# The queue's part between the two pairs of maxima, VectorE held in the source's order, and FP4 quantization in three steps

## The chip, the core and the metric

The kernel runs on one core of a Trainium2 chip. Its engines work side by side, each through its own queue of instructions: PE (TensorE, matmuls, with PEld for the loading of weights), DVE (VectorE), ACT (ScalarE), POOL (GpSimd) and SP (SyncE, which issues most DMAs). The metric is the device time of one execution in microseconds, taken as the median of several runs.

## What is computed

One transformer layer in float32: x has 4 batches of 2048 rows of 256. Attention with 16 heads of 16, residual and layer norm, then a gated feed-forward with FP4 quantization of activations and weights, residual and layer norm.

```python
q, k, v = (split_heads(x @ W.T) for W in (Wq, Wk, Wv))
attn = softmax(einsum('bhld,bhmd->bhlm', q, k) / sqrt(16))
x = layernorm(x + merge(attn @ v) @ Wo.T)
gate, y = fp4_linear(x, w_gate), fp4_linear(x, w_up)       # 256 -> 704
x = layernorm(x + fp4_linear(silu(gate) * y, w_down))      # 704 -> 256
# fp4_linear quantizes both operands in blocks of 16:
scale = max(|block|) / 6;  q = nearest of 0, .5, 1, 1.5, 2, 3, 4, 6 times scale
```

## The kernel before

**Steps and periods.** Attention is cut into 64 steps: a batch, a block of 512 query rows and a group of four heads. A step has 16 periods, so there are 1024 of them, and the loop at L860 writes them out, n from -20 to 1025. Four steps, 64 periods, make a block of query rows. In a period a step gets 128 rows further in each of three stages, which belong to different steps:

- *maxima* (L417), 20 periods ahead (LEAD): the scores of 128 query rows against 512 keys, for a pair of heads at a time. A pair is two matmuls (pm) of 62 rows of contraction, in the two halves of the array. VectorE reduces both banks to row maxima (mx, L432). There are two pairs in a period, here called m0 and m1; pm has two buffers.
- *exponentials* (L458): the transposed scores of 128 keys, two pairs of matmuls (pe) of 64 rows, here e0e1 and e2e3, with ScalarE's exponential after each (e, L466).
- *values* (L469), two periods behind (LAG): av, four heads side by side, eight matmul records.

**The queue's part.** All other work is cut into parts by generators that yield: projections of q, k and v (pq, pv, with transposes ptx), the output projection (py), the feed-forward (ptq, pg, pu, pth, pz) and the preparation of the FP4 weights (`prepare`, L265). `period` (L819) first runs what is due, then the urgent generators (`max_rows`, pn; `normalize`, pa and pr), then as many parts of the queue as are still free: one in a period, two before n = 0. A part counts if it yields at least LEAST = 300. A generator that waits for something also yields LEAST: the period then has no part. On TensorE the part comes last; it is called F here. Each next block's `chain` joins the queue when a block of query rows has its values.

**Due work.** `later(periods, step, rest)` (L117) puts a step into a period to come and returns a test that becomes true `rest` periods after the step ran. `fp4` (L146) uses it: block maxima (amax), scale (sc), its reciprocal (rs) and the scaled rows (xn, on POOL) at once, the rounding (m on VectorE, three operations on POOL) one period later.

**Order.** TensorE's instructions are held in the order of the source by `matmul` and `transpose` (L134, L137). Those of VectorE, ScalarE, POOL and SP are put in order by the framework, from the dependences and its own estimate of when an engine is free.

**Memory.** Three PSUM banks (px) serve pe and all parts in turn, four serve pm, one av. The weights' pieces (wl) have one buffer: ten pieces, loaded by SP in `load` (L278), quantized and transposed into place during the first block. k tiles are loaded in every fourth period, for the step two ahead, into 16 buffers, so SP waits there for the step that is just running.

**The end.** After the loop L900 empties the queue, and `feed_forward_last` (L678) does the last block of rows by itself.

Of the kernel before, what the change touches and what calls it, by code (L numbers as in the profile page):

```python
# [38 lines left out]
P = 128  # L39
# [13 lines left out]
LEAD = 20  # L53
LAG = 2
E_BUFS = 10
LEAST = 300.0
# [15 lines left out]


@with_exitstack
def block_kernel(
# [11 lines left out]
):  # L87
    nc = tc.nc
    B, L, D = x.shape
    FF = w_gate.shape[0]  # L90
# [55 lines left out]
    def fp4(pool, t, tag, gain=1.0):  # L146

        p, nb, _ = t.shape
        amax = pool.tile([p, nb], F32, tag="amax" + tag, name="amax")
        nc.vector.tensor_reduce(amax, t, AX.X, ALU.max, apply_absolute_value=True)  # L150
        sc = pool.tile([p, nb], F32, tag="sc" + tag, name="sc")
        nc.vector.tensor_scalar(sc, amax, gain / 6.0, 1e-12, ALU.mult, ALU.max)
        rs = pool.tile([p, nb], F32, tag="rs" + tag, name="rs")
        nc.vector.reciprocal(rs, sc)
        nc.gpsimd.tensor_scalar(rs, rs, gain * TIES_DOWN, 1.0, ALU.mult, ALU.mult)
        xn = pool.tile([p, nb, FB], F32, tag="xn" + tag, name="xn", bufs=3 if tag else 2)
        nc.gpsimd.tensor_tensor(xn, t, rs.unsqueeze(2).to_broadcast([p, nb, FB]), ALU.mult)

        def rounded():
            m = pool.tile([p, nb, FB], F32, tag="m" + tag, name="m", bufs=1)  # L160
            nc.vector.tensor_single_scalar(m.bitcast(I32), xn.bitcast(I32), EXPONENT, ALU.bitwise_and)
            nc.vector.tensor_scalar(m, m, 1.0, ROUND, ALU.max, ALU.mult)  # L162
            nc.gpsimd.tensor_tensor(xn, xn, m, ALU.add)  # L163
            nc.gpsimd.tensor_tensor(xn, xn, m, ALU.subtract)  # L164
            nc.gpsimd.tensor_tensor(xn, xn, sc.unsqueeze(2).to_broadcast([p, nb, FB]), ALU.mult)  # L165

        return xn, later(1, rounded, 4 if tag == "" else 2)

# [75 lines left out]
    def turn_w(name, dst):  # L244
        for kc in range(KC):
            pt = psum("ptw")
            for n in range(KC):
                transpose(pt[:, n * P : (n + 1) * P], loaded[name][:, n, kc * P : (kc + 1) * P], ident)
            if name == "wv":
                nc.vector.tensor_copy(dst[:, kc, :], pt[:, :D])  # L250
                continue

            for n in range(KC):
                nc.vector.tensor_copy(
                    dst[:, kc, n * P : (n + 1) * P].rearrange("p (d h) -> p d h", h=NC),
                    pt[:, n * P : (n + 1) * P].rearrange("p (h d) -> p d h", h=NC),
                )
# [7 lines left out]
    def prepare():  # L265
# [9 lines left out]
        nc.scalar.copy(woT.rearrange("p k n -> p (k n)"), pt)  # L275
        yield 500

# [36 lines left out]
        for piece, after in zip(pieces, pieces[1:] + [None]):  # L314
            following = load(*after) if after else None
            yield from transposed(*piece, *q)
            q = following
            yield 500

# [13 lines left out]
    def project(b, tb, what):  # L333
# [7 lines left out]
        for kc in range(KC):  # L341
# [4 lines left out]
            yield 600  # L346
        for name, c in [(w[0], int(w[1])) for w in what if w != "v"]:
            w, dst = (wkT, kx[b % 2][c][:, :, rows]) if name == "k" else (wqT, qx[(b * NQB + tb) % len(qx)][c])
# [16 lines left out]
            projected.add((b, tb, name + str(c)))  # L365
        for t in range(QT if "v" in what else 0):
            v = vt[(tb * 2 + t // 2) % 4]
            pv = psum("pv")
            for kc in range(KC):
                matmul(  # L370
                    pv[:, :D], xT[:, kc, t * P : (t + 1) * P], wvT[:, kc, :], start=(kc == 0), stop=(kc == KC - 1)
                )
            src = pv[:, :D].rearrange("p (g i j d) -> p g i j d", g=NG, i=NP, j=2)
            for j in range(2):
                nc.scalar.copy(v[:, :, t % 2, :, 2 * j * DH : (2 * j + 1) * DH], src[:, :, :, j, :])
            if t % 2:
                t0 = tb * QT + t - 1
                nc.sync.dma_start(
                    vx[b % 2][:, :, t0 : t0 + 2, :].rearrange("g p t c -> p g (t c)"),
                    v.rearrange("p g t i c -> p g (t i c)"),  # L380
                )
            if t == QT - 1:
                projected.add((b, tb, "v"))
            yield 900

# [31 lines left out]
    def maxima(s, n, i):  # L417
# [5 lines left out]
        for j in range(2):  # L423
# [7 lines left out]
            )  # L431
        nc.vector.tensor_reduce(mx_sb[s][:, t, 2 * i : 2 * i + 2, kb], pm, AX.X, ALU.max)  # L432

    def max_rows(s):

        nm = p2.tile([P, QT, HG], F32, tag="nm", name="nm")
        nc.vector.tensor_reduce(nm, mx_sb.pop(s), AX.X, ALU.max, negate=True)
        nh = p2.tile([P, QT, HG, 2], F32R, tag="nh", name="nh")
        nc.vector.tensor_copy(nh[:, :, :, 0], nm)
        nc.vector.tensor_tensor(nh[:, :, :, 1], nm, nh[:, :, :, 0].bitcast(F32), ALU.subtract)  # L440
        yield 0
# [15 lines left out]

    def exponentials(s, kt, i):  # L458
        kb, col = kt // QT, kt % QT * P
        pe = [psum("pe") for _ in range(2)]  # L460
        for j in range(2):
            rows = slice(R * j, R * j + R)
            matmul(pe[j], k_sb[s, i, kb][rows, col : col + P], q_sb[s, i][rows, :], start=True, stop=True)
        for j in range(2):
            e = p1.tile([P, QB], F32, tag="e", name="e", bufs=E_BUFS)
            nc.scalar.activation(e, pe[j], AF.Exp, scale=SCALE)  # L466
            e_sb[s, kt, 2 * i + j] = e

# [14 lines left out]
    def normalize(s):  # L483
# [10 lines left out]
        rd = p2.tile([P, QT, NP, 2], F32, tag="rd", name="rd")  # L494
        nc.vector.reciprocal(rd, pairs[:, :, :, 1:3, 0])
        if s % 2 == 0:
            oq_of[s // 2] = p2.tile([P, QT, P], F32, tag="oq", name="oq", bufs=1)
        oq = oq_of[s // 2].rearrange("p t (g i j d) -> p t g i j d", g=2, i=NP, d=DH)
        for i in range(NP):
            nc.vector.tensor_tensor(  # L500
                oq[:, :, s % 2, i],
                pairs[:, :, i, 0:4:3, :],
                rd[:, :, i, :].unsqueeze(3).to_broadcast([P, QT, 2, DH]),
                ALU.mult,
            )
        yield 500
        if s % 2 == 0:
# [7 lines left out]
        oTs[s // 2] = oT  # L515
        yield 500


    def layer_norm(r, t0, n):

        mv = p2.tile([P, n, 2], F32, tag="mv", name="mv")
        for t in range(n):
            st = p2.tile([P, 6], F32, tag="st", name="st")
            nc.vector.bn_stats(st, r[:, t0 + t, :])  # L524
            nc.vector.bn_aggr(mv[:, t, :], st)
        rstd = p2.tile([P, n], F32, tag="rstd", name="rstd")
# [9 lines left out]
    def residual(b, qb, x1, xq):  # L536

        for t in range(QT):
# [10 lines left out]
            if t % 2:  # L549
                layer_norm(x1, t - 1, 2)  # L550
                tiles = x1[:, t - 1 : t + 1].rearrange("p t (b f) -> p (t b) f", f=FB)
                later(3, lambda tiles=tiles: xq.append(fp4(p2, tiles, "")))
            yield 900
# [35 lines left out]
    def turned(hq, tiles, hT):  # L589
# [4 lines left out]
        for t in range(2):  # L594
# [3 lines left out]
            nc.scalar.copy(hT[:, t, :4, :].rearrange("p c n -> p (c n)"), pt)  # L598
            yield 500
        pt = psum("pth").rearrange("p (t c n) -> p t c n", t=2, c=2)  # L600
# [4 lines left out]
        for c in range(4, NFC):  # L605
            w = min(P, FF - c * P)
            nc.scalar.copy(hT[:w, :, c, :], pt[:w, :, c - 4, :])
        yield 500

# [10 lines left out]
    def feed_forward(b, qb, between):  # L620
# [13 lines left out]
        for kc in range(KC):  # L634
# [4 lines left out]
            nc.scalar.copy(xqT[:, kc, :], pt)  # L639
            yield 500  # L640
        hq = {}

        def gate(t):
            h = p2.tile([P, FF], F32, tag="h", name="h")
            yield from gated(xqT, h, t)
            blocks = h.rearrange("p (b f) -> p b f", f=FB)
            later(1, lambda: hq.update({t: fp4(p2, blocks, "h", gain=0.5)}))

        def out_rows(t):
            layer_norm(x1, t, 2)  # L650
            at = slice(qb * QB + t * P, qb * QB + (t + 2) * P)
            nc.sync.dma_start(out[b, at, :].rearrange("(t p) d -> p t d", p=P), x1[:, t : t + 2, :])

# [164 lines left out]

    def period(parts):  # L819

        take_due()
        for _ in range(len(urgent)):
# [36 lines left out]

    for n in range(-LEAD, N + LAG):  # L860
        m = n + LEAD
        (sm, im), (s, kt), (sv, kv) = divmod(m, NKT), divmod(n, NKT), divmod(n - LAG, NKT)
        if m in (8, 10, 12, 14):
# [3 lines left out]
        if n == 0:  # L867
            load_v(0)
        if n == N - NKT:
            x1_last = load_last(*steps[-1][:2])  # L870
        if kt == 3 and 0 <= n and s + 1 < len(steps):
# [11 lines left out]

        for i in range(NP):
            if m < N:
                maxima(sm, im, i)
        for i in range(NP):
            if 0 <= n < N:
                exponentials(s, kt, i)
            if i == 0 and n >= LAG:  # L890
                values(sv, kv)
        if m < N and im == NKT - 1:
            urgent.append(max_rows(sm))
        if n >= LAG and kv == NKT - 1:
            urgent.append(normalize(sv))
            if sv % NG == NG - 1 and sv + 1 < len(steps):
                queue.append(chain(*steps[sv][:2]))
        period(1 if n >= 0 else 2)
    banks["more"] = True
    while urgent or queue or due:  # L900
        period(1)
    feed_forward_last(*steps[-1][:2], x1_last)
# [32 lines left out]
```

## Time and profile before

| what | value |
|---|---|
| runs | 3656.62 us median (3651.92 to 3656.71) |
| profiled execution | 3651.45 us, span 3649.4 us |
| DVE busy with mx | 2408.6 us of 2816.2, 1217 ns each |
| ACT busy with e | 2218.8 us of 2691.0 |
| first av group, last av group | 99.19 us, 3571 us |

The trace can be cut into periods at each start of an av group. Sorted by the part F that a period has:

| part in the period | periods | us, median |
|---|---|---|
| pz | 120 | 3.855 |
| pu, pg | 240 | 3.71 |
| pq, pv, py | 217 | 3.39 |
| pth, ptq, pa, pn, pr, ptx, ptw | 318 | 3.09 |
| none | 127 | 2.65 |

Within a class they differ by about 0.3%, except among the first 64 periods, where single ones take up to 10.6 us.

The parts of a block of 64 periods, in order of time (y py, x ptx, q pq, t ptq, g pg, u pu, v pv, h pth, z pz; N, A and R are pn, pa and pr, urgent; a point is a period without a part):

```
.A.RyyyyxxqNqqqttAguguqqgugNuqqguAgRuvvhhhgNuguvvAzzzzhhhzzNzz..     eleven such blocks
.A.Ryyyy...N...ttAgugugugugNuguhhAhRguguzzzNzhhhzAzzz.........       the last one
```

How to read the rows of the trace: a timeline row has the start in us, the busy time, engine, line, operation, output <- inputs and how many were merged; brackets give the idle time before it and what ended it. A row of waits has who waited for whom, then the total in us, the number of times, and the longest. For overlapping matmuls the distance between starts tells more than the durations, since matmul ends are modelled.

### The profile page before, as it was taken

Reading aid. Unit: us, or ns where it says so; the run is one execution under the profiler, and the core shown is the slowest. Engines: PE = TensorE matmul, PEld = TensorE weight load, DVE = VectorE, ACT = ScalarE, POOL = GpSimd, SP = SyncE. Lnnn points to the kernel's source line nnn. Section 1 sums busy time; section 2 is a strip of 40 time slices with the busy share of each in tenths; the row PEclk is TensorE's granted clock in tenths of the full one; section 3 lists DMA queues with packets and bytes.
Section 4 is the critical chain, followed back from the end, with each engine's and each line's share of the span. In section 5 each row is a group of like instructions: output and inputs, shape, how many; then the busy total and the mean of one; then the engine's idle time right before and its main releaser. Section 6 shows DMA issues by size and latency. Waiting matters only on the chain.

```text
span 3649.4 us, 57772 instructions
## 1 busy us (share of the span) xinstructions
PE 3534.1 (97%) x21348; PEld 1593.8 (44%) x21348; DVE 2816.2 (77%) x3310; ACT 2691.0 (74%) x5446; POOL 1251.3 (34%) x1496
## 2 busy tenths in 40 slices
PE   7889999999999999999999999999999999999996
PEld 5333444444444444444444444444443434444343
DVE  5777778787787778778787787878778787888845
ACT  3677777777777777777777777777777777777772
POOL 1331423434243242424324243342424325142430
PEclk9999999999999999999999999999999999999998
DMA  6533323323232322323223232322322221222100
GB/s 219 164 123 99 119 68 113 89 85 103 82 98 87 105 84 83 116 68 116 85 85 106 80 100 86 97 85 83 109 69 77 67 84 50 86 66 81 57 21 6
DMA packets 190640, 328.39 MB, mean 90 GB/s; under 512 B 24344, under 2 KB 68248, under 8 KB 190360
## 3 DMA queue, kind: packets, MB, share of 16 engines
q1 hardware_dynamic: 188968, 323.39, 29.1%
q8 instruction: 171, 2.80, 0.3%
q10 hardware_dynamic: 1392, 1.31, 0.1%
q14 instruction: 109, 0.89, 0.1%
HBM read 237.04 MB, written 86.51 MB: 89 GB/s over the span
## 4 chain that ended last, share of the span: by engine, by line
PE 82%; DVE 12%; DMA 2%; POOL 2%; issue 1%; ACT 1%; SPq 0%; POOLq 0%; ACTq 0%; DVEq 0%
PE av L135 24%; PE pe L135 18%; PE pm L135 16%; DVE mx L432 9%; PE pz L135 6%; PE pg L135 5%; PE pu L135 5%; PE pq L135 3%; PE pv L135 2%; PE pth L138 1%; PE pa L138 1%; PE py L135 1%; PE pn L138 1%; DMA qx<-qhi 1%; DVE st L524 1%
## 5 line engine op out<-in xcount | busy, mean ns | idle before, releaser
L432 DVE TENSOR_REDUCE mx<-pm 128x2 f32<-128x1024 f32 x2048 | 2408.6, 1217 | 666.5 <-PE pm L135 662.2
L466 ACT ACTIVATE e<-pe 128x512 f32<-128x512 f32 x4096 | 2218.8, 596 | 676.0 <-PE pe L135 670.8
L135 PE MATMUL av<-e,v 128*32 128x512 f32 x8192 | 1098.0, 608 | 4.2 <-DMA v<-vx 4.2
L135 PE MATMUL pe<-q,k 64*128 64x512 f32 x4096 | 1036.4, 456 | 4.9 <-ACT e L466 4.5
L135 PEld LDWEIGHTS pe<-q,k 64*128 64x128 f32 x4096 | 476.6, 184 | 968.5 <-ACT e L466 853.8
L135 PE MATMUL pm<-k,q 62*128 62x512 f32 x4096 | 805.1, 448 | 67.1 <-DVE mx L432 57.5
L135 PEld LDWEIGHTS pm<-k,q 62*128 62x128 f32 x4096 | 346.8, 185 | 382.7 <-DVE mx L432 178.2
L135 PEld LDWEIGHTS av<-e,v 128*32 128x32 f32 x8192 | 162.1, 108 | 335.5 <-issue 312.9
L572 POOL TENSOR_TENSOR a<-a,g 128x352 f32<-128x352 f32 x120 | 112.6, 938 | 494.5 <-ACT a L571 494.5
L135 PE MATMUL pz<-wdT,hT 128*128 128x128 f32 (+1 forms) x1488 | 233.4, 299 | 1.5 <-ACT hT L757 1.5
L617 POOL TENSOR_TENSOR x<-x,read 128x128 f32<-128x128 f32 x120 | 54.8, 456 | 482.2 <-ACT read L143 482.2
L135 PEld LDWEIGHTS pz<-wdT,hT 128*128 128x128 f32 x1488 | 190.5, 193 | 50.5 <-ACT e L466 18.2
L163 POOL TENSOR_TENSOR xn<-xn,m 128x704 f32<-128x704 f32 (+2 forms) x100 | 153.6, 1536 | 153.5 <-DVE m L162 131.6
L586 POOL TENSOR_TENSOR h<-a,u 128x352 f32<-128x352 f32 x120 | 112.4, 937 | 226.0 <-ACT u L585 224.0
L135 PE MATMUL pg<-wgT,xqT 128*128 128x352 f32 x512 | 186.5, 487 | 1.9 <-ACT xqT L720 1.9
L135 PE MATMUL pu<-wuT,xqT 128*128 128x352 f32 x512 | 185.0, 484 | 0.0
L548 POOL TENSOR_TENSOR x<-x,read 128x256 f32<-128x256 f32 x60 | 43.8, 730 | 374.0 <-ACT read L143 374.0
L164 POOL TENSOR_TENSOR xn<-xn,m 128x704 f32<-128x704 f32 (+2 forms) x100 | 153.8, 1538 | 5.4
L165 POOL TENSOR_TENSOR xn<-xn,sc 128x704 f32<-128x704 f32 (+2 forms) x100 | 126.4, 1264 | 7.5
L573 POOL TENSOR_TENSOR a<-a,g 128x352 f32<-128x352 f32 x120 | 113.9, 949 | 9.4
L135 PEld LDWEIGHTS pg<-wgT,xqT 128*128 128x128 f32 x512 | 87.5, 190 | 60.2 <-ACT e L466 19.1
L135 PEld LDWEIGHTS pu<-wuT,xqT 128*128 128x128 f32 x512 | 87.6, 189 | 58.1 <-ACT e L466 20.0
(114 smaller groups left out, 2278.8 us busy)
## 6 DMA issues: line engine op xcount, KB each, us to landing
k<-kx SPq DMA_DIRECT2D x1024, 128.0 KB
v<-vx SPq DMA_DIRECT2D x64, 768.0 KB
q<-qx SPq DMA_DIRECT2D x256, 124.0 KB
kx<-khi SPq DMA_DIRECT2D x64, 256.0 KB
qx<-qhi SPq DMA_DIRECT2D x64, 256.0 KB
vx<-vt SPq DMA_DIRECT2D x32, 384.0 KB
xb<-in_L_attn_x_dram SPq DMA_DIRECT2D x16, 512.0 KB
kx<-klo SPq DMA_DIRECT2D x32, 256.0 KB
```

The lines of the kernel that those rows point to most:

```text
L135: tc.keep_in_program_order(nc.tensor.matmul(*args, **kw))
L138: tc.keep_in_program_order(nc.tensor.transpose(*args))
L163: nc.gpsimd.tensor_tensor(xn, xn, m, ALU.add)
L164: nc.gpsimd.tensor_tensor(xn, xn, m, ALU.subtract)
L165: nc.gpsimd.tensor_tensor(xn, xn, sc.unsqueeze(2).to_broadcast([p, nb, FB]), ALU.mult)
L432: nc.vector.tensor_reduce(mx_sb[s][:, t, 2 * i : 2 * i + 2, kb], pm, AX.X, ALU.max)
L466: nc.scalar.activation(e, pe[j], AF.Exp, scale=SCALE)
L548: nc.gpsimd.tensor_add(x1[:, t, :], x1[:, t, :], read(py[:, :D]))
L572: nc.gpsimd.tensor_mul(a, a, g)
L573: nc.gpsimd.tensor_add(a, a, g)
L586: nc.gpsimd.tensor_mul(h[:, cols], a, u)
L617: nc.gpsimd.tensor_add(x1[:, t, cols], x1[:, t, cols], read(pz))
```

## The change

1. **The part's place.** The body of a period follows the list ORDER: m0, the queue's parts (`more`), m1, then the due work, e0, e1, av, e2, e3. `exponentials` does one head at a time and takes one bank at a time. `max_rows` and `normalize` start at once where they become possible (`begin` runs them to their first yield).
2. **VectorE's order.** Instructions of VectorE in the loop go through the wrapper InOrder, which holds them in the order of the source. Those of `feed_forward_last` and `fp4_at_once` don't.
3. **FP4 in three steps.** amax at once; sc, rs and xn one period later; rounding three periods later. The two layer norms in the loop run two periods later instead of at once; the FP4 of the normalised rows is due four periods after that instead of three, that of h three instead of one.
4. The projection takes its parts in the order given (k0, q0, v, k1, q1) and not with v last. Some yields of 500 become 600.

```diff
+ORDER = "m0 q m1 e0 e1 v e2 e3".split()
...
+class InOrder:
...
+    def __getattr__(self, name):
+        return lambda *args, **kw: self.tc.keep_in_program_order(getattr(self.engine, name)(*args, **kw))
...
-        nc.vector.tensor_reduce(amax, t, AX.X, ALU.max, apply_absolute_value=True)
+        vector.tensor_reduce(amax, t, AX.X, ALU.max, apply_absolute_value=True)
...
+        def scaled():
+            vector.tensor_scalar(sc, amax, gain / 6.0, 1e-12, ALU.mult, ALU.max)
+            rs = pool.tile([p, nb], F32, tag="rs" + tag, name="rs")
+            vector.reciprocal(rs, sc)
+            nc.gpsimd.tensor_scalar(rs, rs, gain * TIES_DOWN, 1.0, ALU.mult, ALU.mult)
+            nc.gpsimd.tensor_tensor(xn, t, rs.unsqueeze(2).to_broadcast([p, nb, FB]), ALU.mult)
...
-        return xn, later(1, rounded, 4 if tag == "" else 2)
+        later(1, scaled)
+        return xn, later(3, rounded, 4 if tag == "" else 2)
...
-    def exponentials(s, kt, i):
+    def exponentials(s, kt, h):
+        i, j = divmod(h, 2)
         kb, col = kt // QT, kt % QT * P
-        pe = [psum("pe") for _ in range(2)]
...
+        pe = psum("pe")
...
-                layer_norm(x1, t - 1, 2)
-                tiles = x1[:, t - 1 : t + 1].rearrange("p t (b f) -> p (t b) f", f=FB)
-                later(3, lambda tiles=tiles: xq.append(fp4(p2, tiles, "")))
+
+                def normed(t=t):
+                    layer_norm(x1, t - 1, 2)
+                    tiles = x1[:, t - 1 : t + 1].rearrange("p t (b f) -> p (t b) f", f=FB)
+                    later(4, lambda: xq.append(fp4(p2, tiles, "")))
+
+                later(2, normed)
...
-            later(1, lambda: hq.update({t: fp4(p2, blocks, "h", gain=0.5)}))
+            later(3, lambda: hq.update({t: fp4(p2, blocks, "h", gain=0.5)}))
...
-        for i in range(NP):
-            if m < N:
-                maxima(sm, im, i)
-        for i in range(NP):
-            if 0 <= n < N:
-                exponentials(s, kt, i)
-            if i == 0 and n >= LAG:
-                values(sv, kv)
-        if m < N and im == NKT - 1:
-            urgent.append(max_rows(sm))
...
-        period(1 if n >= 0 else 2)
+        for step in ORDER:
+            if step[0] == "m" and m < N:
+                maxima(*divmod(m, NKT), int(step[1]))
+                if step == "m1" and (m + 1) % NKT == 0:
+                    begin(max_rows(m // NKT))
+            if step == "m1":
+                take_due()
+            elif step == "q":
+                more(1 if n >= 0 else 2)
+            elif step[0] == "e" and 0 <= n < N:
+                exponentials(*divmod(n, NKT), int(step[1]))
+            elif step == "v" and n >= LAG:
+                s, kt = divmod(n - LAG, NKT)
+                values(s, kt)
...
```

## The prediction

> **What bounds the kernel now.** First the page: which engine is full, and at which clock.
>
> ```profile
> PE 3534.1 (97%) x21348; PEld 1593.8 (44%) x21348; DVE 2816.2 (77%) x3310; ACT 2691.0 (74%) x5446; POOL 1251.3 (34%) x1496
> ...
> PE   7889999999999999999999999999999999999996
> ...
> PEclk9999999999999999999999999999999999999998
> ...
> PE 82%; DVE 12%; DMA 2%; POOL 2%; issue 1%; ACT 1%; SPq 0%; POOLq 0%; ACTq 0%; DVEq 0%
> ```
>
> TensorE is full except in the first three slices (some 270 us) and the last. DVE has 12% of the chain of waits, which looks like a prize of 438 us, so the second view is one ordinary period in the timeline:
>
> ```profile
> 1005.52 0.50 PE L135 MATMUL pe<-q,k 64*128 64x512 f32 x2
> 1005.95 1.13 PE L135 MATMUL py<-woT,oT 128*128 128x256 f32 x4
> 1007.01 0.74 PE L135 MATMUL pm<-k,q 62*128 62x512 f32 x4
> 1007.57 0.42 PE L135 MATMUL pe<-q,k 64*128 64x512 f32 x2
> 1007.92 1.07 PE L135 MATMUL av<-e,v 128*32 128x512 f32 x8
> 1008.91 0.50 PE L135 MATMUL pe<-q,k 64*128 64x512 f32 x2
> ```
>
> From start to start: e2e3 0.43, the part 1.06, both pairs of maxima 0.56, e0e1 0.35, av 0.99. Nothing is idle between them. The periods with a part of one kind hardly differ (60 of py: 3.376 to 3.400), so VectorE's work of the loop already hides. The chain's DVE share is a walk through two engines that are both busy. So I expect nothing from a smoother VectorE in those periods.
>
> Third, where VectorE itself waits, before 300 us:
>
> ```profile
> DVE mx L432 <- PE pm L135: 38.3, 28, 6.8
> DVE amax L150 <- DMA wl<-in_L_ffn_w_down_dram: 7.6, 1, 7.6
> DVE amax L150 <- DMA wl<-in_L_ffn_w_up_dram: 7.3, 2, 6.4
> DVE amax L150 <- DMA wl<-in_L_ffn_w_gate_dram: 3.9, 3, 3.2
> ```
>
> The block maxima of the weights' FP4 wait 18.8 us for their loads. Fourth, one of these on three engines (SP's, VectorE's and TensorE's timelines):
>
> ```profile
> 226.98 0.43 SPq L281 DMA_DIRECT2D wl<-in_L_ffn_w_down_dram  x1
> ```
>
> ```profile
> 224.98 1.22 DVE L432 TENSOR_REDUCE mx<-pm 128x2 f32<-128x1024 f32 x1
> 233.81 0.89 DVE L150 TENSOR_REDUCE amax<-wl 128x44 f32<-128x704 f32 x1 [7.62 <-DMA wl<-in_L_ffn_w_down_dram]
> 234.61 2.35 DVE L432 TENSOR_REDUCE mx<-pm 128x2 f32<-128x1024 f32 x2
> ```
>
> ```profile
> 235.88 0.80 PE L135 MATMUL pm<-k,q 62*128 62x512 f32 x2 [6.27 <-DVE mx L432]
> ```
>
> amax stands in VectorE's queue ahead of two maxima, its load was issued at 226.98 and is used at 233.81, and TensorE stands 6.27 us. **Here VectorE's order costs time.**
>
> **Part 1: the part between the pairs.** The order on TensorE was m0 m1 e0e1 av e2e3 F; it becomes m0 F m1 e0e1 av e2e3. In a circle only one thing happens: m0 moves from behind F to ahead of it, and joins e2e3. The Trainium skill, "TensorEngine Tiling (Array Packing)", Key Properties, says that changing the tiling mode drains TensorE, which speaks against splitting a run of 64-row matmuls. Row: a pair alone, e2e3 ahead of F, takes 0.428 (1005.52 to 1005.95); three pairs in a run, m0 m1 e0e1, take 0.911 (1007.007 to 1007.918), so an inner pair costs 0.23. Were the split one more lone pair, it would cost 0.2 in each of 895 periods with a part, 179 us. But the drains per period stay four (into F, out of F, into av, out of av): one run of one and one of three become two runs of two. A run of two is in the trace in a period without a part:
>
> ```profile
> 2078.42 0.40 PE L135 MATMUL pm<-k,q 62*128 62x512 f32 x2
> 2079.17 0.50 PE L135 MATMUL pm<-k,q 62*128 62x512 f32 x2 [0.35 <-DVE mx L432]
> 2079.51 0.41 PE L135 MATMUL pe<-q,k 64*128 64x512 f32 x2
> 2079.84 0.64 PE L135 MATMUL av<-e,v 128*32 128x512 f32 x4
> ```
>
> m1 to av is 0.67. Before 0.428 + 0.911 = 1.339, after 2 x 0.67 = 1.34: **nothing**, within 5 ns a period either way (5 us in all, in the range).
>
> The 318 periods with a short part (0.59: transposes) take 3.09, where 2.316 + 0.585 = 2.90 would do. There e1 waits for its score bank, the third of three, until e3's exponential of the period before ends, 1.67 after e2e3 starts; 127 periods without a part take 2.60 to 2.65 by the same chain. Allocating the banks singly leaves their order and the four exponentials the same: nothing. ScalarE reads F's bank in 0.37 to 0.92 and must free it and e0's before e2e3, 1.67 after F ends; the longest, g (copy at 0.16, tanh until 0.98), puts e0's exponential at 0.89 to 1.48: 0.19 spare, nothing.
>
> VectorE in a period: m0's maximum may start 0.5 after m0, m1's 0.5 after m1; both take 2.43 of 3.4 to 3.7. The buffer of m1 is wanted again about 1.5 after its maximum ends. Dues placed there are below that: layer_norm 1.2 (2 x 0.41 + 2 x 0.18), rounded 1.05 (0.52 + 0.53), amax 0.88, sc and rs 0.65. Two dues in a period delay maxima, not TensorE. If that cover failed by 1 us at each of the 60 FP4s of h, it would cost 60 us (a rival).
>
> Before the first exponential (36 to 88 us) two parts go in a period, and three periods take 7.9 (46.45 to 54.36) where two of them are filled by TensorE at 2.59 and the third by VectorE at 2.43: 7.6. A part no longer queues behind m1's wait. Bounds 0 and 5 x 0.3; I take **-1.5**.
>
> **Part 2: three steps, and later ones.** No instruction is added: POOL's, ScalarE's and SP's are the same, later. Stepping through the yields, the normalised rows' transposes become ready 13 periods after the fourth py instead of 8, and h's 9 after its last u instead of 5. A block of 64 periods had 4 to spare, so each chain runs over into the next block, until its lateness meets the idle periods there. In all 3 of the 120 pz fall behind the loop. Saved in it 3 x (3.855 - 2.605) = 3.75; added after it: 3 x 1.33 on TensorE, in part in its waits there (0.68 ahead of pa, 0.88 ahead of pr), and a layer_norm of 1.2 on VectorE: +2.5 (bounds 0 and 5.2). **Net -1.** The yields of 500 that become 600 are both above LEAST: nothing.
>
> **Part 3: VectorE in the source's order.** This decides. Counting av groups from the first (period n = 2, at 99.19), the amax that waited at 175.19 runs at n = 22, and its piece is loaded in the source at n = 25; that of 233.81 runs at 38 for 42. So the framework had put them ahead of maxima that come earlier in the source, and SP, behind k loads, had not fetched them. With the order held, they stand behind those maxima and, with parts counted anew, at n = 32 and 46; their loads wait only for the xn of the piece before, 7 and 4 periods earlier (13 us or more, against 3.0 to 7.4 from issue to use). What each cost, as excess of its periods over their kind: 6.02 + 0.97 at 170 to 184, 7.55 + 0.79 at 227 to 242 (the second of each at a lower clock after the stall): **-15.3**. The first two pieces (6.2 at 113 to 129) are loaded in the source at n = 5 and 7, where they ran already: unchanged. Late next: a piece two periods behind another (n = 7, 34) and the large one at 46, behind k loads of n = 44: +1.5, between 0 and 3 x 3.
>
> **Sum.** -15.3 + 1.5 - 1.5 - 1 = -16.3 against the profiled execution's 3651.45 (span 3649.4), so 3635; the median of the runs is 5.2 above that execution, so 3656.6 - 16 = **3641**.
>
> **Rivals.**
> - No change: the loads' landing is what is late, and the stalls only move. For it: they are seven of 3656 us each, and SP's queue stays the framework's. Parts 1 and 2 alone: 3654.
> - Slower: ten amax, each fixed behind m0's maximum, hold m1's maximum if SP issues wl only when TensorE gets there. Issue to use about 4, less 1.0 to spare, ten times, plus 4 for each of the three at n = 16, 20, 32, which share their period with k loads: 42 against 21.5 now: 3677. It decides if wl is issued less than about 3 us ahead of its amax. Against it: SP issued the fifth piece at 149.2, some six periods ahead of the source. The same sort of wait on POOL's xn at `rounded` would give 3717; two periods for an xn of 1.39 speak against it.
> - Faster by more: the bank chain of the 318 short periods opens (0.19 each): 3641 - 60 = 3581. The unchanged order of banks speaks against it.
>
> **Chances.** Forecast 0.57, no change 0.20, slower 0.17 (0.13 and 0.04), the large gain 0.06. The forecast's own range is 3630 to 3649: all 21.5 of stalls gone and the small terms good, or half of the 15.3 lost. The range takes in the no-change case and half of the slower one: 3625 to 3668. A measurement of this kernel can tell some 0.2% (7 us) from no change. The forecast is beyond that in nine cases of ten: faster 0.57 x 0.9 + 0.06 + a twentieth for the no-change case's edge = 0.62, same 0.20, slower 0.18.
>
> **What will show it.** Right: amax's waits for wl fall from 18.8 to below 9, the 6.3 us waits of TensorE for mx near 170 and 227 are gone, and py periods stay at 3.39. Wrong in part 1, if py periods move by over 0.02; in part 2, if more than three pz follow the last av; in part 3, if VectorE waits for wl as long as before, or for POOL's xn in the loop.

## The result, and the profile after

| | before | after |
|---|---|---|
| median of 6 runs, us | 3653.28 (3651.92 to 3656.71) | 3630.48 (3627.14 to 3634.2) |
| ratio | | 0.9935 [0.9922, 0.9948] |
| profiled execution, us (span) | 3651.45 (3649.4) | 3627.21 (3625.4) |
| first av | 99.2 | 98.7 |
| first 64 periods | 234.6 | 233.1 |
| the next 704 | 2404.5 | 2381.5 |
| the rest of the loop | 832.4 | 831.4 |
| from the start of the last av group | 78.7 | 80.7 |

The kernel is 23 us faster; a gain of 16 and a time of 3641 were forecast. The lower rows cut the span at starts of av groups: 23.0 of the 24.0 us come from the 704 periods behind the first 64, and 1.5 from those 64, where 13.8 had been forecast. The page of the changed kernel, first its busy times, then the shares of its chain of waits:

```profile
PE 3531.5 (97%) x21348; PEld 1531.6 (42%) x21348; DVE 2859.1 (79%) x3310; ACT 2677.8 (74%) x5446; POOL 1248.7 (34%) x1496
...
PE 88%; DVE 8%; DMA 2%; issue 1%; ACT 1%; SPq 0%; POOL 0%; POOLq 0%; ACTq 0%; DVEq 0%
```

The numbers of instructions and TensorE's 97% are the same: nothing was taken out. DVE is even busier by 43 us, and yet its share of the chain fell from 12% to 8%. The view that finds the gain is one that the prediction does not show: whom TensorE waits for between 340 and 3500 us, first before, then after (total us, times, longest):

```profile
PE pm L135 <- DVE mx L432: 37.1, 85, 0.8
```

```profile
PE pm L148 <- DVE mx L83: 16.9, 38, 1.3
```

37.1 us in 85 small waits became 16.9 in 38. About the same amount comes out of the periods. With each period set against the mean of its kind before, periods 66 to 1005 are 21.5 us shorter in all: ptx 11.4 (22 periods), those without a part 8.9, pq 3.3, ptq 1.2; no other kind moved by more than 1.6.

What a ptx period did before, in VectorE's timeline and then TensorE's:

```profile
1013.54 0.43 DVE L524 BATCH_NORM_STATS2 st<-x 128x6 f32<-128x256 f32 x1 [0.24 <-POOL x L548]
1013.89 0.67 DVE L150 TENSOR_REDUCE amax<-x 128x32 f32<-128x512 f32 x1
...
1014.59 0.58 DVE L152 TENSOR_SCALAR sc<-amax 128x32 f32<-128x32 f32 x1
...
1015.76 1.20 DVE L432 TENSOR_REDUCE mx<-pm 128x2 f32<-128x1024 f32 x1
```

```profile
1016.11 0.66 PE L138 MATMUL ptx<-ident,xb 128*128 128x128 f32 x4
1017.02 0.51 PE L135 MATMUL pm<-k,q 62*128 62x512 f32 x2 [0.25 <-DVE mx L432]
1018.21 0.50 PE L135 MATMUL pm<-k,q 62*128 62x512 f32 x2 [0.69 <-DVE mx L432]
```

Behind the fourth py of every block, the framework put a layer norm and a whole FP4 head (amax, sc, rs), 2.2 us from 1013.54 on, between two maxima. Both maxima were then late, and the two pairs of the next ptx period stood 0.25 and 0.69: 4.2 us instead of 3.1. VectorE after, at the same place of a block:

```profile
1673.81 0.18 DVE L83 BATCH_NORM_AGGREGATE mv<-st 128x2 f32<-128x6 f32 x1
1673.91 2.40 DVE L83 TENSOR_REDUCE mx<-pm 128x2 f32<-128x1024 f32 x2
```

The layer norm now stands by itself (1672.83 to 1673.99), with the maxima right behind it; the FP4 head comes periods later. ptx periods take 3.09 to 3.19.

The py period that the prediction showed, after the change, in TensorE's timeline:

```profile
1676.52 0.40 PE L148 MATMUL pm<-k,q 62*128 62x512 f32 x2
1676.85 1.13 PE L148 MATMUL py<-woT,oT 128*128 128x256 f32 x4
1677.91 0.51 PE L148 MATMUL pm<-k,q 62*128 62x512 f32 x2
1678.25 0.40 PE L148 MATMUL pe<-q,k 64*128 64x512 f32 x2
```

m0 stands ahead of the part, 0.33 from start to start, and m1 0.34 behind it. The two runs of two pairs cost what one and three did: py periods have a mean of 3.391, and had 3.388.

The stalls in the first block moved. The two pieces of the weights that the prediction priced wait no longer. The sixth (6.37 at 175.19 before) is issued at 187.24, and the ninth (7.62 at 233.81 before) at 253.40; VectorE then takes both without a wait:

```profile
205.61 0.67 DVE L83 TENSOR_REDUCE amax<-wl 88x32 f32<-88x512 f32 x1
...
262.63 0.88 DVE L83 TENSOR_REDUCE amax<-wl 128x44 f32<-128x704 f32 x1
```

Other pieces wait instead. VectorE's waits for the weights between 94 and 300 us (total us, times, longest):

```profile
DVE amax L83 <- DMA wl<-in_L_ffn_w_gate_dram: 10.7, 2, 8.7
DVE amax L83 <- DMA wl<-in_L_ffn_w_up_dram: 10.7, 1, 10.7
DVE amax L83 <- DMA wl<-in_L_ffn_w_down_dram: 0.5, 1, 0.5
```

They sum to 21.9, against 18.8 before. The first piece has 8.7 of it, where it had 3.2; the seventh has 10.7, where it had none. The seventh on POOL, on SP's queue and on VectorE:

```profile
208.27 1.05 POOL L172 TENSOR_TENSOR xn<-wl,rs 88x512 f32<-88x512 f32 x1
```

```profile
210.28 2.11 SPq L379 DMA_DIRECT2D qx<-qlo  x2
212.49 0.50 SPq L300 DMA_DIRECT2D wl<-in_L_ffn_w_up_dram  x1
213.65 0.59 SPq L437 DMA_DIRECT2D v<-vx  x1
```

```profile
222.83 0.68 DVE L83 TENSOR_REDUCE amax<-wl 88x32 f32<-88x512 f32 x1 [10.66 <-DMA wl<-in_L_ffn_w_up_dram]
```

VectorE stood from 212.17 on, before the load was even issued. The one buffer was free at 209.32, when POOL's xn of the sixth piece ended; SP came to the load 3.2 us later, behind copies to qx, and from its issue to its use 10.3 us passed. The first piece was issued at 106.14, 3.0 us before VectorE stood for it, and was used 11.7 after its issue.

### The profile page after: what moved, and what is told of

The parts are those of the page before. It is cut to its first block, busy times and chain, and to the rows that moved or that the text cites. A ratio compares the mean times of both kernels' runs of the same rounds, so it can differ in the third digit from the quotient of the medians.

```text
span 3625.4 us, 57726 instructions
## 1 busy us (share of the span) xinstructions
PE 3531.5 (97%) x21348; PEld 1531.6 (42%) x21348; DVE 2859.1 (79%) x3310; ACT 2677.8 (74%) x5446; POOL 1248.7 (34%) x1496
## 4 chain that ended last, share of the span: by engine, by line
PE 88%; DVE 8%; DMA 2%; issue 1%; ACT 1%; SPq 0%; POOL 0%; POOLq 0%; ACTq 0%; DVEq 0%
PE av L148 25%; PE pe L148 19%; PE pm L148 17%; PE pz L148 6%; DVE mx L83 6%; PE pg L148 5%; PE pu L148 5%; PE pq L148 3%; PE pv L148 2%; PE py L148 2%; PE pth L151 1%; PE pa L151 1%; PE pn L151 1%; DVE m L83 1%; DMA wl<-in_L_ffn_w_gate_dram 1%
## 5 line engine op out<-in xcount | busy, mean ns | idle before, releaser
L83 DVE TENSOR_REDUCE mx<-pm 128x2 f32<-128x1024 f32 x2048 | 2456.6, 1221 | 617.9 <-PE pm L148 533.2
L148 PE MATMUL pe<-q,k 64*128 64x512 f32 x4096 | 1050.1, 458 | 3.7 <-ACT e L487 2.7
L148 PE MATMUL pm<-k,q 62*128 62x512 f32 x4096 | 934.2, 446 | 48.1 <-DVE mx L83 40.9
L148 PEld LDWEIGHTS pm<-k,q 62*128 62x128 f32 x4096 | 409.1, 186 | 339.6 <-DVE mx L83 179.0
L156 ACT COPY read<-pz 128x128 f32<-128x128 f32 x120 | 31.8, 265 | 112.1 <-PE pm L148 103.6
```

What stands on the lines that cost most here:

```text
L83: return lambda *args, **kw: self.tc.keep_in_program_order(getattr(self.engine, name)(*args, **kw))
L148: tc.keep_in_program_order(nc.tensor.matmul(*args, **kw))
L156: nc.scalar.copy(t, bank)
```

## The experiments

Three things can be switched: the part's place (P), VectorE's held order (O), and the times of FP4 and of the layer norms (S). Some runs switch one on alone, some take one out of the changed kernel, and the rest settle a detail. Ratios are to the kernel before, with the 95% interval. "The loop" is periods 66 to 1005 like for like, in us against before (after: -21.5).

**Order alone.** Before, with `nc.vector` held in the loop:

```diff
+    vector = InOrder(tc, nc.vector)
...
-        nc.vector.tensor_reduce(amax, t, AX.X, ALU.max, apply_absolute_value=True)
+        vector.tensor_reduce(amax, t, AX.X, ALU.max, apply_absolute_value=True)
```

> The kernel before, with VectorE held in the source's order and nothing else. Theory S (the steps of FP4 and the later norms make the gain, by taking layer norm, amax, sc and rs out of one period): the ptx period behind the fourth py stays near 4.2 us, since the source itself has layer norm and FP4 there; 3645 to 3665. Theory V (the framework's order put small work ahead of maxima, and holding the order makes the gain): ptx periods fall to 3.1 us and the time by 15 us or more, to below 3640.

Measured: 3696.38, ratio 1.0112 [1.0098, 1.0126], slower than either theory had it; the loop +48.9, TensorE's waits for mx 69.1 in 152. In VectorE's waits from 340 to 3500 us one row has grown, from 3.9 us in 15 before:

```profile
DVE st L81 <- POOL x L559: 46.3, 30, 1.8
```

The source has the layer norm right behind the residual sum, which POOL makes. Held there, bn_stats stands for POOL 30 times, 1.5 us each, with the maxima queued behind it. The framework's reordering had hidden most of this. Holding the order is no gain of itself, and a wait that an in-order queue meets is paid by all behind it.

**Steps alone.** Before, with the new times (`scaled` one period later, `rounded` three, the norms two), the projection in the order given, and no held order:

```diff
+        later(1, scaled)
+        return xn, later(3, rounded, 4 if tag == "" else 2)
...
+                later(2, normed)
```

> The kernel before, with FP4 in three steps and the later norms (and v in the projection's given order, without which the lateness leaves v too late); part last, VectorE free. Theory S: ptx 3.1 us, pq 3.39, the periods of the loop 15 to 22 us shorter in all, 3630 to 3640. Theory V or P (the part's place): under 7 us, 3647 to 3657.

Measured: 3661.95, 1.0016 [1.0009, 1.0022], above both expectations. The loop gains 6.2 (periods without a part 12.2, ptx 3.7; pq loses 2.4), and the first 64 periods lose 16.0 (250.6), where the weights' amax waits 25.1 for wl. Later steps are no gain by themselves either.

**Place alone.** The new body of the period, with the old times and VectorE free:

```diff
+    vector = nc.vector
...
+ORDER = "m0 q m1 e0 e1 v e2 e3".split()
```

> The body of a period as after (m0, part, m1), with FP4 and norms timed as before and VectorE free. Theory P (the gap between the two maxima takes up VectorE's small work): ptx periods near 3.1 us, 3630 to 3640. Theory S or V: ptx still 3.9 to 4.2 us, py 3.39, 3645 to 3660.

Measured: 3678.59, 1.006 [1.0047, 1.0074], above both expectations; the loop +28.3. ptx and the periods without a part gain 10.0 and 11.1, but pn and pg lose 13.8 each, pz 12.2, pu 5.4. In TensorE's waits, pg and pz now wait for ScalarE's e (10.2 and 5.5 us, at most 0.4 each), and pn for VectorE's nh (5.7 us in 4). The periods right behind a pa lose 19.7 us in 59; why, the next but one shows. What else pn loses was not followed further.

**Norms alone.** Before, with only the layer norms two periods later and their FP4 four after that (and the projection in the order given):

```diff
-                layer_norm(x1, t - 1, 2)
...
+                later(2, normed)
```

> The kernel before, with only the attention's layer norm two periods later and its FP4 six after the row (and v in the given order). If the pile of layer norm, amax, sc and rs behind the fourth py is the whole of the loop's loss at ptx and pq: ptx 3.1 us, 13 to 15 us less, 3637 to 3642. If the pieces merely meet again elsewhere: under 5 us, 3649 or more.

Measured: 3680.44, 1.0066 [1.0053, 1.0078]; the loop +24.0: ptx -4.3, but pq +14.9 and pth +15.3. The pile was moved and met others. At 1704.16 the framework put m ahead of a ready maximum, and m waited 1.89 us for POOL's xn; and in 12 of the 64 steps nh's CAST took 1.65 to 1.71 us (see the end).

**The changed kernel with VectorE free.**

```diff
-    vector = InOrder(tc, nc.vector)
+    vector = nc.vector
```

> The kernel after, with VectorE's order left to the framework. Theory S: within 7 us of after, 3624 to 3638. Theory V: most of the gain is lost, 3645 or more. In the first block the amax of the weights would wait as before (near 19 us) or less.

Measured: 3679.33, 1.0067 [1.0055, 1.008]; the loop +19.2 (pz +11.1, pu +6.3, pn +4.3). The periods right behind a pa lose 22.2 us in 59; in the changed kernel they gain 1.7. One pa and what follows it, with VectorE free, in VectorE's timeline, then TensorE's:

```profile
1762.05 0.25 DVE L516 RECIPROCAL rd<-pa 128x16 f32<-128x16 f32 x1
1762.21 1.17 DVE L454 TENSOR_REDUCE mx<-pm 128x2 f32<-128x1024 f32 x1
1763.29 0.47 DVE L521 TENSOR_TENSOR oq<-pa,rd 128x128 f32<-128x128 f32 x2
```

```profile
1763.57 0.45 PE L148 MATMUL pm<-k,q 62*128 62x512 f32 x2
1764.41 1.45 PE L148 MATMUL pu<-wuT,xqT 128*128 128x352 f32 x4 [0.40 <-ACT e L487]
```

The same place of a block in the changed kernel, where the order is held:

```profile
1735.52 0.25 DVE L83 RECIPROCAL rd<-pa 128x16 f32<-128x16 f32 x1
1735.80 0.49 DVE L83 TENSOR_TENSOR oq<-pa,rd 128x128 f32<-128x128 f32 x2
```

```profile
1737.03 0.39 PE L148 MATMUL pm<-k,q 62*128 62x512 f32 x2
1737.35 1.45 PE L148 MATMUL pu<-wuT,xqT 128*128 128x352 f32 x4
```

Left free, oq, the last reader of pa's bank, was put behind the second maximum. It ends 2.97 us after pa starts (1760.79), and 2.03 when held (pa at 1734.26). With pa's bank still taken, the next period has two banks for its scores, and its part has to wait until ScalarE has read one of them: it starts 0.84 behind its pair of maxima, and 0.32 when held. All 51 periods with a part behind a pa do this (0.85 in the median, against 0.33), and so do the 44 of the run with the place alone (0.85). That ScalarE's e releases the part is in the trace; which bank it is, is my reading. With the part at the end of the period and VectorE free (steps alone), the periods behind a pa lose nothing (-0.2).

**Only the maxima and the normalization held.** As the last, but `mx`, `rd` and `oq` go through InOrder:

```diff
+    held = InOrder(tc, nc.vector)
+    vector = nc.vector
...
+        held.tensor_reduce(mx_sb[s][:, t, 2 * i : 2 * i + 2, kb], pm, AX.X, ALU.max)
```

> The kernel after, with VectorE free (as in e5, 3679 us), except that the maxima and normalize's rd and oq are held in the source's order among themselves. In e5 the period before a pa takes 0.52 us more, four times a block, and rd and oq run behind the second maximum there, with pa's score bank still to be read. If this late reading is what the free order costs: the 0.5 us at pa go, some 59 x 0.52 = 31 us, 3643 to 3653. If the free order costs through other things: 3665 or more.

Measured: 3662.43, 1.0028 [1.0017, 1.0038], between the two expectations; the loop +9.2. Of the 40.7 us that a free VectorE costs the loop, 10.0 come back. oq again ends 2.03 after pa starts in the median, and the periods behind a pa (behind, not before it as expected) lose 9.5 instead of 22.2. So that reading is right for part of it; what is left lies in other kinds too (pz +5.9, pn +4.2, pa +3.2).

**The part last, all else as changed.**

```diff
-ORDER = "m0 q m1 e0 e1 v e2 e3".split()
+ORDER = "m0 m1 e0 e1 v e2 e3 q".split()
```

> The kernel after, with the part behind e3 again (m0 m1 e0 e1 v e2 e3 q; the due work stays behind m1). Theory S or V: within 7 us of after, 3624 to 3638, py 3.39. Theory P: 3640 or more.

Measured: 3643.99, 0.9971 [0.9961, 0.9982]; the loop -8.9; TensorE's waits for mx 34.5 in 83. ptx keeps its gain (-10.2), and the periods without a part lose theirs (+0.8). The place is worth some 13 us here, though the matmuls themselves cost the same. My reading, which no run isolates: with the part between the pairs the two pairs start 1.39 us apart (1676.52 and 1677.91) and not together, so a late maximum holds up one pair and not both.

**The old times, all else as changed.**

```diff
-        later(1, scaled)
-        return xn, later(3, rounded, 4 if tag == "" else 2)
+        return xn, later(1, rounded, 4 if tag == "" else 2)
...
-                later(2, normed)
```

> The kernel after, with FP4 in two steps and the norms and FP4 timed as before. Theory S: ptx near 4.2 us again and the gain gone, 3645 to 3660. Theory V or P: within 7 us of after.

Measured: 3659.86, 1.0018 [1.0011, 1.0024]; the time that theory S had; the loop +12.4 (pn +13.3, pz +6.1, while ptx keeps -7.2 and does not go back to 4.2). From 1680.40 to 1682.39 VectorE runs nm, nh, nh, amax, sc and rs in one row, since all fall due in the same period, and TensorE pays:

```profile
1683.61 0.51 PE L148 MATMUL pm<-k,q 62*128 62x512 f32 x2 [0.60 <-DVE mx L83]
```

This is a pile again, of the FP4 head and nm and nh, and here the source itself puts them together.

**FP4 in two steps, with the late norms kept.** As changed, with the first three lines of that diff only:

> The kernel after, with sc, rs and xn together with amax and the rounding one period later, but the norms and FP4 due as late as after. If the late norms are what counts of the third part: within 7 us of after, 3623 to 3638. If it is the three steps: 3645 or more, with waits of pm for mx at periods that have amax, sc and rs together.

Measured: 3642.31, 0.997 [0.9959, 0.9982], between the two expectations; the loop -4.1 (ptx -12.0, but pu +5.7 and periods without a part +3.7). ptx keeps its gain, so the third step is not needed for it; that step is worth some 13 us beside it.

**Order and late norms, the part last, FP4 in two steps**, to see whether late norms take away what held order costs:

> The kernel before with VectorE held (as in e1, 3696 us) and with the layer norms two periods later and the FP4 of their rows four after that; FP4 itself in two steps as before. In e1 the held bn_stats wait 46 us for POOL's sum of the residual. If that wait is what the held order costs alone: st's waits fall under 5 us and the time to 3640 to 3660. If FP4's steps matter as much: 3665 or more.

Measured: 3689.17, 1.0099 [1.0085, 1.0113]; the loop +43.5. The waits of bn_stats for POOL are gone, as is the loss in py and pq (-0.1 and -3.9), yet pth loses 32.4 and pn 12.7. One such period, 2.4 us too long in eleven blocks, in VectorE's timeline, then TensorE's:

```profile
1805.29 0.53 DVE L81 TENSOR_SCALAR m<-m 128x704 f32<-128x704 f32 x1
1805.73 0.21 DVE L81 TENSOR_REDUCE nm<-mx 128x16 f32<-128x64 f32 x1
1805.98 1.70 DVE L81 CAST nh<-nm 128x16 fp32r<-128x16 f32 x1
```

```profile
1809.08 0.51 PE L146 MATMUL pm<-k,q 62*128 62x512 f32 x2 [1.64 <-DVE mx L81]
```

The rounding of h falls into the period in which max_rows starts, and CAST waits for POOL. One pile is undone and another made.

**The weights a piece ahead.** The changed kernel with two wl buffers; each load is issued one piece earlier, amax stays:

```diff
-                t = p2.tile([P, FF], F32, tag="wl", name="wl", bufs=1)
+                t = p2.tile([P, FF], F32, tag="wl", name="wl", bufs=2)
...
-        for piece, after in zip(pieces, pieces[1:] + [None]):
-            following = load(*after) if after else None
+        for n, piece in enumerate(pieces):
+            if n + 2 < len(pieces):
+                coming.append(load(*pieces[n + 2]))
+            following = fp4(p2, *coming.popleft()) if coming else None
```

> The kernel after, with two buffers for the weights' pieces, so that each load is issued one piece earlier, while its amax stays where it is. If amax in the held order waits for loads that were issued too late: the waits of amax for wl fall from 21.9 us to under 6, the first 64 periods from 233 to 213 to 220 us, 3610 to 3620. If the loads are slow because DMA queues are full at that time: the waits stay above 12 us, 3622 to 3634.

Measured: **3610.81**, 0.9881 [0.9867, 0.9894], faster than both kernels. VectorE's wait for weights between 94 and 300 us is one row:

```profile
DVE amax L83 <- DMA wl<-in_L_ffn_w_gate_dram: 0.3, 1, 0.3
```

The first 64 periods take 211.5, 21.6 less than after; the loop is unchanged (-22.2). So an issue one piece earlier, with the second buffer that it needs, takes the stalls away; which of the two does it, no run isolates. The loads themselves are no faster: the second piece is issued at 111.00 and used at 121.23, 10.2 us later. The first load now lies at 5.19, among the loads of the start, and the first av group comes at 103.0 instead of 98.7. Whether a later place for it gives these 4 us too was not tried.

The eight ways to switch O, S and P, in us against before (the ratio less one, times 3655):

| | P off | P on |
|---|---|---|
| neither | 0 | +22 |
| S | +6 | +24 |
| O | +41 | +7 |
| O and S | -11 | **-24** |

One difference runs beside the switches: in the column with P off, the first three rows have the period's body of before, with the due work just ahead of the queue's part; the last row has the new body, with the part moved to its end and the due work behind m1.

## Why the prediction was right, and where not

The time fell into the range and the sign is right, but by luck: the first block, which was to give nearly all of the 16 us, gave 1.5, and the loop behind it, which was to give next to nothing, gave 21.5.

- **Part 3, -15.3 + 1.5: failed, measured -1.5** (the whole of the first 64 periods). The -15.3 came, by the path foreseen: both pieces are issued 18.4 and 9.2 us ahead of their amax and wait no longer. Two other terms failed. The first pieces were "loaded in the source at n = 5 and 7, where they ran already: unchanged"; the first had run a period later, at n = 6, and held at n = 5 its amax waits 8.7 instead of 3.2. And "a piece two periods behind another (n = 7, 34)" was among those priced at +1.5, "between 0 and 3 x 3"; the one of n = 34 alone waits 10.7. It had one buffer that came free 2.9 us before VectorE wanted the piece, SP issued it 3.2 later still, and it took 10.3 to arrive, where 3.0 to 7.4 had been read from the trace. This is the first rival in the first block: "the loads' landing is what is late, and the stalls only move". The slower rival's condition, wl issued less than about 3 us ahead of its amax, held for the seventh piece and just about for the first (3.0); its price of 42 was twice the 21.9 of waits. The weights moved ahead show what was to be had: without these waits the first 64 periods are 21.6 shorter.
- **"VectorE's work of the loop already hides ... I expect nothing": failed, measured -21.5.** This is nearly the whole gain. It was read from medians and from 60 py, whose spread was small indeed. But other periods differ by far more than the 0.3% told ahead of the prediction, behind the first 64 too: of 22 ptx, eleven take 4.18 to 4.20, in a class whose median is 3.09; eleven of 88 pq take 3.72 to 3.75; and those without a part, told as 2.60 to 2.65, reach 4.27. A stall once in a block is invisible in the median of a class of 318; the mean of ptx, 3.64, shows it. The row of TensorE's own waits, 37.1 us in 85, was in the trace too. That the chain's DVE share is no price was right: its fall from 12% to 8% is some 145 us, six times the gain. That nothing lay under it was wrong.
- **Part 1, nothing: right for TensorE** (medians of py 3.388 and 3.391, of pz 3.855 and 3.860; 5 ns was the bound). The lone pairs would have been 179 us. (From the figures shown, an inner pair costs 0.24, not 0.23; nothing hangs on it.) But "nothing" was the price of the place on one engine; alone it costs 22 us, and within the whole it is worth 13. With the part last TensorE's waits for mx double, to 34.5; with the place alone the parts wait for ScalarE and the bank. "Two dues in a period delay maxima, not TensorE" is the sentence that the runs with the old times refute.
- **Part 2, net -1: right in its pieces.** Three pz fall behind the loop (117 of 120 in it, and 132 periods without a part instead of 128), and the time from the last av on grew by 2.0 (2.5 was taken). But the later steps were counted only as lateness of the queue. What they do for VectorE's queue, 30 us by the run without them, was not in the sum.
- **The start, -1.5: measured -0.5.**
- **The bank chain opening:** it did not; pn, pa and pth kept 3.09 to 3.10.

Of the four signs that were named, three came as said: py's 3.39, the three pz, and the end of TensorE's waits for mx near 170 and 227 (on TensorE 4.6 and 6.3 us; one of 10.5 now ends at 224.7). amax's waits rose to 21.9 instead of falling below 9; that was named as the sign against part 3, and it decided so. The waits for POOL's xn that the slower rival priced came to 4.6 us, once, behind 340 us.

What the experiments show as the cause: none of the three edits is a gain alone, and taking one out of the whole costs some 13 (place), 30 (times) and 48 us (order), by the differences of the ratios, each within about 7 us. Held order without the late norms has VectorE stand for POOL in its own queue (46.3 us at bn_stats), and with late norms and FP4 in two steps it has the rounding of h meet nh's CAST. The place without held order has the framework put a bank's last reader behind a maximum. The steps without held order gain 6.2 in the loop and lose 16.0 in the first block, where the weights' amax wait. Still open: the rest of the loss with VectorE free (9.2 with maxima and oq held, against -21.5), the loss at pn with the place alone, and what makes up the part of the 48.9 of held order alone that is not in TensorE's waits for mx, which account for 32 more than before.

## What to carry to other kernels

Where the full engine feeds on another that is 79% busy, ask for the full engine's own waits over the steady stretch before calling the other one hidden: medians by kind hide what happens once in a block. An order held by hand pays only if each instruction's inputs are ready at its place, so steps are moved apart first, and both are tried together; a try of one alone would have rejected each of them here. And a load stands in its issuer's queue: to have it earlier, move its issue and give it a buffer. The time from issue to use is to be read from the slow cases (here 10 to 12 us), not from the usual ones.

## What the runs showed of the hardware

- **CAST stands for POOL.** nh's CAST (128x16) takes 0.175 to 0.177 us in the changed kernel wherever POOL is idle. Beside POOL's two-input operations it ends 0.03 us after they do: 1.697 to 1.705 in eleven steps of the run with order and late norms, of which 1.665 to 1.672 lay beside `xn<-xn,m`; 0.75 to 0.78 in the kernel before, beside 0.71 to 0.74. Beside POOL's small rstd it took 0.176 to 0.179, nearly as usual. The Trainium skill, "SBUF — State Buffer", Who interferes with whom, says that a copy or cast in a mode of two ports and GpSimd take a shared pair of ports for the whole instruction, and whoever comes second fully blocks; these lengths agree with it, to 0.03 us; in which mode CAST runs, no view shows.
- **A small load among large ones.** The seventh piece, 176 KB, was in use 10.3 us after its issue at 212.49, with v's 768 KB issued 1.2 us later. In the changed kernel the first piece took 11.7, with two loads of 512 KB (xb) issued from 3.1 us later on, and the fourth 11.3, with v's 1.7 us later; the second was in use 3.5 after its issue, without a wait. In the kernel before, pieces took 3.0 to 7.4. That the large loads are the reason was not tried.
- **The clock in and behind a stall.** In the changed kernel TensorE stands for the seventh piece from 214.2 to 224.7. Its granted clock is 1.00 from 214 to 216 us, 0.50 from 216 to 228, and 1.00 again from 230 on; the av at 225.85 takes 1.93 us, where the next takes 1.06. In the kernel before, the clock was 0.50 from 176 to 180, at the end of the stall for the sixth piece and behind it, and 1.00 from 182 on. The two periods with the stall of 10.5 take 14.0 and 4.8 us, 12.6 over the 3.09 of their kinds.
